# Fixed slots for the lane stages of a convolution, Mamba, attention and experts kernel

## The chip, the cores and the metric

The kernel runs on one core of a Trainium2 chip. The metric is the device time of one execution in microseconds (us). The median of three runs of the kernel before is 5564.33 us (5563.74 to 5565.13).

## The reference

The input x has 4 images of 128 channels and 64x64 pixels, in float32. Two layers follow each other. Cut to what matters:

```python
# layer 0, on the group-normed x, channels last; added to x
xn  = ln(x);  y = xn + fc2(gelu(ln(conv3x3_depthwise(xn))))
u   = ln(y)                                    # 4 chunks of 32 channels, one Mamba each
xin, z = split(u @ in_proj.T);  xin = silu(conv1d(xin))
dt, Bm, Cm = split(xin @ x_proj.T)             # 16 states
delta = softplus(dt @ dt_proj.T + b)
h_t = exp(delta*A) * h_(t-1) + delta*Bm*xin    # along 4096 pixels
m   = (sum_n h*Cm + D*xin) * silu(z) @ out_proj.T + skip*u
x   = x + ln(xn + m) @ proj.T + b
# layer 1, tokens of 128 channels
t = t + attention(ln(t))                       # 4 heads, 4096 x 4096 scores per image
t = t + top2_of_8_experts(ln(t))
```

## The kernel before, in words

An image is cut into NB = 8 blocks of BLK = 512 pixels, so there are 32 blocks. The Mamba scan of one block is 2 halves of 128 partitions (p) with NST = 16 states (n) each. One such (block, p, n) is a unit, and the main loop (lines 1223 to 1270) takes one unit in each turn. A turn is called a slot: 32 slots to a block, 1024 in all. The order in which each engine gets its instructions is the order in which this Python code emits them: `queued` (line 428) ties each instruction to the one before it on its engine.

A slot emits, in this order:

1. `fetched` (732), the DMA of the rows B and C for the unit three slots ahead, on SP; the copy of the last scan's end state, on ACT; `decayed` (742), the exp `da` for the unit two slots ahead, on ACT.
2. One group of attention (line 943): two key tiles of 128 against 1024 queries, that is 4 matmuls `sc` on PE and 2 exps `pT` of 128x1024 on ACT. The matmuls of the probabilities with the values (`weighted`, 960: 8 matmuls `av`) come in the next slot.
3. `scan` (747) on DVE: `h` = rows times `du`, the scan over `h`, and `hc` = rows times `h`. From slot ALONE = 128 (line 1220) on, two neighbours' `hc` are added on POOL, and PE adds the sum into `y`, once in two slots (line 1257).
4. Stages of two lanes, X and Y. All the rest of the work hangs on them. A task is a generator, and each `yield` ends half a stage. `advance(lane, second)` (1137) runs one half: in each slot the second half of X (line 1250, so that of the stage begun in the slot before), the first half of Y, then the `y` matmul, the second half of Y (1263), the `av` matmuls of the group before, and the first half of X (1267). So a lane does one stage per slot, mostly PE in one half and DVE or ACT in the other.

The tasks of Y, for block k, stand in a queue filled ahead (lines 1190 to 1208): `in1` = `inputs(k, p=1)` (3 stages), `y0` = `first_norm(k+2)` (5 stages), `xn` = `conv(k+1)` (13 stages), `in0` = `inputs(k+1, p=0)` (3 stages); at the end of an image also `group_norm` (539). The tasks of X are `closed(k)` (769, 11 stages: output projection, two layer norms, q, k, v of the attention), put in front as soon as block k is scanned (line 1262), and `finished` (1010, called "out", 16 stages: one block of attention output, router, experts), which may begin only in slots 2 to 17 of a block (lines 1148 to 1152). `in1` of block k waits for the scan of block k-1, that is for slot 1 of block k; `in0` of the next block waits for the scan of half p=0, slot 17. `inputs` and `closed` exclude each other by `held` (683, 798). Each lane has one PSUM bank for its matmuls (`work`, 487).

Which task is next is asked in `advance`; apart from the gates above a lane runs as fast as one stage per slot:

```python
if tasks[0][0][0] == "out" and slot < len(units) + 4 and not 2 <= slot % (2 * NST) < NST + 2:
    return False
key, stages, _ = tasks.popleft()
running[lane] = key, stages(lane) if callable(stages) else stages
```

`until` (1165) runs both lanes without slots where an input is needed at once (three slots ahead, line 1227). After slot 1023 the rest of the attention and of the `out` tasks runs alone.

Inside the stages, these names matter: `normalised` (502) is 4 bn_stats and 4 bn_aggr on DVE (`st`, `mv`), then 4 small operations on POOL (`rs`, `shift`), a half without work, and 4 scalings of 128x128 on ACT (`xt`). `inputs` (679) has matmuls in its first stage, then `xin` and `zs` (silu) on ACT with a table load on either side; in its second stage more matmuls, then `bc`, `e`, `ln`, `delta` on ACT, again with two table loads; in its third five operations on POOL (lines 721 to 725, ending in `du`). `conv` does the 9 taps on DVE for images 1 to 3 (line 623), on PE for image 0. In `finished`, `aT` (1025) is multiplied on DVE and used by 4 matmuls with `wp`; the router's top-2 search (1070 to 1078) is 16 small operations on DVE whose result `pr` is transposed on PE; four pairs of experts take a `share` on DVE and a pair of matmuls each (1115 to 1126).

Of the kernel before, what the change touches and what calls it, by code (L numbers as in the profile page):

```python
# [24 lines left out]
NST = 16  # L25
# [11 lines left out]
def conv_mamba_attn_moe_kernel(ctx: ExitStack, tc: tile.TileContext, t: dict):  # L37
    nc = tc.nc
    x, out = t["x"], t["out"]
    B, _, L = x.shape  # L40
    NB = L // BLK
# [61 lines left out]
    with (  # L103
# [20 lines left out]
        for i, (w, bias) in enumerate(((wqn, bqn), (wkn, bkn))):  # L124
            for h in range(NH):
# [9 lines left out]
                k = NH * i + h  # L135
# [10 lines left out]
        norm = bd.tile([1, 2 * NH + 1], F32, name="norm")  # L146
# [317 lines left out]
    def flush():  # L464
        for entry in outgoing:
            entry[0] -= 1
            if entry[0] == 0:
                sync.dma_start(out=entry[1], in_=entry[2])
        outgoing[:] = [entry for entry in outgoing if entry[0]]
# [69 lines left out]
    def group_norm(b):  # L539

        gst = small.tile([P, NB, 6], F32, name="gst", bufs=1)
        ahead = [load_x(x[b], i, "xg") for i in range(2)]
        yield
        yield
        for i in range(0, NB, 2):
            now = ahead
            if i + 2 < NB:
                ahead = [load_x(x[b], i + 2 + u, "xg") for u in range(2)]
            yield
            for u in range(2):  # L550
                vector.bn_stats(out=gst[:, i + u, :], in_=now[u])
            yield
        gmv = small.tile([P, 2], F32, name="gmv", bufs=1)
        vector.bn_aggr(out=gmv, in_=gst)
        ps = work("Y")
        mm(ps[:, 0:1], gmat, gmv[:, 0:1])
        yield
        gm = small.tile([P, 1], F32, name="gm", bufs=2)
        vector.tensor_copy(gm, ps[:, 0:1])
        gd = small.tile([P, 1], F32, name="gd", bufs=1)  # L560
        vector.tensor_sub(gd, gmv[:, 0:1], gm)
        gv = small.tile([P, 1], F32, name="gv", bufs=1)
        vector.scalar_tensor_tensor(gv, gd, gd, gmv[:, 1:2], ALU.mult, ALU.add)
        yield
        ps = work("Y")
        mm(ps[:, 0:1], gmat, gv)
        yield
        gr = small.tile([P, 1], F32, name="gr", bufs=2)
        vector.tensor_scalar_add(gr, ps[:, 0:1], EPS)
        gpsimd.tensor_tensor(gr, gr, mhalf[:, 0:1], ALU.pow)  # L570
        group_of[b] = gm, gr
        yield

    def first_norm(b, i, lane):

        gn = load_x(x[b], i, "gn")
        yield
        gm, gr = group_of[b]
        yield
        yield  # L580
        vector.tensor_scalar(gn, gn, gm, gr, ALU.subtract, ALU.mult)
        yield
        ps = transposed(lane, by_tile(gn))
        yield
        xt = yield from normalised(lane, by_tile(ps))
        ps = transposed(lane, xt).rearrange(IMAGE, w=IMG)
        yield
        y0 = mix.tile([P, ROWS + 2, IMG + 2], F32, name="y0", bufs=4)
        gpsimd.memset(y0[:, :, 0:1], 0.0)
        gpsimd.memset(y0[:, :, IMG + 1 : IMG + 2], 0.0)  # L590
        inner = slice(1, 1 + IMG)
        scalar.activation(y0[:, 1 : 1 + ROWS, inner], ps, AF.Identity, bias=lnb, scale=lnw)
        if i == 0:
            gpsimd.memset(y0[:, 0, inner], 0.0)
        else:
            above = y0_of[b, i - 1]
            scalar.activation(
                above[:, ROWS + 1, inner], ps[:, 0, :], AF.Identity, bias=lnb, scale=lnw
            )
            gpsimd.tensor_copy(y0[:, 0, inner], above[:, ROWS, inner])  # L600
        if i == NB - 1:
            gpsimd.memset(y0[:, ROWS + 1, inner], 0.0)
        y0_of[b, i] = y0
        yield
# [528 lines left out]
    lanes, done, running = {"X": deque(), "Y": deque()}, set(), {}  # L1133

    inside = {"X": False, "Y": False}

    def advance(lane, second):

        if inside[lane] != second:
            return False  # L1140
        while True:
            if lane not in running:

                tasks = lanes[lane] if lanes[lane] or slot < len(units) else lanes["X"]
                if not tasks or not all(k in done for k in tasks[0][2]):
                    return False

                if (
                    tasks[0][0][0] == "out" and slot < len(units) + 4
                    and not 2 <= slot % (2 * NST) < NST + 2  # L1150
                ):
                    return False
                key, stages, _ = tasks.popleft()
                running[lane] = key, stages(lane) if callable(stages) else stages
            key, stages = running[lane]
            try:
                next(stages)
                inside[lane] = not second
                return True
            except StopIteration:  # L1160
                assert not second
                done.add(key)
                del running[lane]

    def until(key):
        while key not in done:
            flush()
            count = len(done)
            moved = [
                advance(*half) for half in (("X", True), ("Y", False), ("Y", True), ("X", False))  # L1170
            ]
            assert any(moved) or len(done) > count, key

    blocks = [(b, i) for b in range(B) for i in range(NB)]

    def before(k, n):

        return [("freed", *blocks[k - n])] if k >= n else []
# [3 lines left out]
    def upper(k):  # L1182
        b, i = blocks[k]
        if i == 0:
            Y.append((("group", b), group_norm(b), []))
        if k != 1:
            Y.append((("y0", b, i), first_norm(b, i, "Y"), before(k, 4)))

    X.append((("y0", *blocks[1]), first_norm(*blocks[1], "X"), [("y0", *blocks[0])]))
    for k in range(-2, len(blocks)):  # L1190
        if 0 <= k:
            b, i = blocks[k]
            Y.append((("in", b, i, 1), inputs(b, i, 1), [("scan", *blocks[k - 1], 1)] if k else []))
        if k + 2 < len(blocks):
            b, i = blocks[k + 2]
            if k + 2 == 0 or i > 0:
                upper(k + 2)
        if 0 <= k + 1 < len(blocks):
            b, i = blocks[k + 1]
            below = [("y0", b, i + 1)] if i < NB - 1 else []  # L1200
            Y.append((("xn", b, i), conv(b, i), before(k + 1, 3) + below))
            Y.append((
                ("in", b, i, 0), inputs(b, i, 0),
                before(k + 1, 2) + ([("scan", *blocks[k], 0)] if k >= 0 else []),
            ))

        if 0 < k + 2 < len(blocks) and blocks[k + 2][1] == 0:
            upper(k + 2)
# [9 lines left out]
    units = [(b, i, p, n) for b, i in blocks for p in range(2) for n in range(NST)]  # L1218

    ALONE = NB // 2 * 2 * NST  # L1220
    rows, decays, old, due = {}, {}, None, deque()
    even, y_of, waiting, slot = None, {}, None, 0
    while slot < len(units) or due or waiting or left or later or lanes["X"] or running:
        flush()

        for ahead in range(slot if slot == 0 else slot + 3, min(slot + 4, len(units))):
            until(("in", *units[ahead][:3]))
            rows[ahead] = fetched(*units[ahead])
# [7 lines left out]
        group = next(groups, None)  # L1236
        if slot < len(units):
# [3 lines left out]
            b, i, p, n = unit  # L1241
# [5 lines left out]
            else:  # L1247
                gpsimd.tensor_add(even, even, hc)
                due.append((slot + 2, unit, even, n == 1))
        advance("X", True)  # L1250
        advance("Y", False)
        while due and due[0][0] <= slot:
            _, unit, term, first = due.popleft()
            b, i, p, n = unit
# [22 lines left out]
    with tc.If(nc.values_load(general[0:1, 0:1]) > 0):  # L1277
# [4 lines left out]
        with tc.For_i(0, B, 1) as b:  # L1282
# [3 lines left out]
                out=t_tok.rearrange("p k c -> p (k c)"),  # L1286
# [97 lines left out]
```

## Time and profile before

| what | value |
|---|---|
| median of the runs | 5564.33 us |
| profiled execution, its own time | 5562.85 us |
| its span, first to last instruction | 5561.1 us |
| busy: PE, DVE, ACT, POOL | 4907.1, 4182.2, 3897.4, 2208.9 us |
| granted TensorE clock, mean | 0.951 |
| slots 0 to 1023 (first to last scan on DVE) | 102.8 to 4969.2 us |
| a block, blocks 8 to 29 | 146.5 to 170.8 us, mean 158.9 us |
| attention groups left after the last slot | 136 of 1024 |

Times are of one profiled execution; "idle before" is the time an engine stood still just before an instruction and the releaser is what it had waited for. Nearly all instructions bear line 445, the helper that records the order, so groups are told apart by the names of their tiles. A slot is found in the trace by its `da` on ACT, its `h` on DVE, and its four `sc` on PE. DVE and ACT may be ahead of PE or behind it in slots.

### The profile page before, as it was taken

How to read it: one execution, taken by the hardware profiler on the slowest of the kernel's cores; microseconds unless marked ns; L12 is line 12 of the kernel's file. 1: busy time of each engine (PE TensorE's matmuls, PEld its weight loads, DVE VectorE, ACT ScalarE, POOL GpSimd, SP SyncE). 2: the span in 40 equal slices, each digit the busy share in tenths (PEclk: the TensorE clock that was granted, in tenths of full speed). 3: DMA queues.
4: the chain of work that ended last, by engine and by line, in shares of the span. 5: the costliest groups of instructions: out<-in, count | busy, mean ns of one | idle time of the engine just before them, and what ended most of it. 6: DMA issues, size and time to landing. Idle time of an engine off the chain costs nothing.

```text
span 5561.1 us, 61179 instructions
## 1 busy us (share of the span) xinstructions
PE 4907.1 (88%) x17866; PEld 2045.2 (37%) x17866; DVE 4182.2 (75%) x6275; ACT 3897.4 (70%) x5989; POOL 2208.9 (40%) x1917
## 2 busy tenths in 40 slices
PE   4667798999899899999999999999899899999997
PEld 2223333333333333333333333333333333344443
DVE  4888778888887888888888888887888788862221
ACT  3455677788777777777877777777777777765553
POOL 2333445445434445444544444444544444421100
PEclk7778899999999999999999999999999999999998
DMA  2456566666665667667765667667765666754542
GB/s 92 169 172 193 185 205 230 215 222 229 228 206 192 228 201 255 216 204 243 249 208 193 209 214 242 219 210 234 249 207 196 207 221 203 249 193 168 168 146 67
DMA packets 451704, 1131.52 MB, mean 203 GB/s; under 512 B 51985, under 2 KB 135330, under 8 KB 451362
## 3 DMA queue, kind: packets, MB, share of 16 engines
q1 hardware_dynamic: 450194, 1126.74, 60.6%
q8 instruction: 144, 2.36, 0.2%
q14 instruction: 198, 1.62, 0.1%
q10 hardware_dynamic: 1168, 0.80, 0.0%
HBM read 967.12 MB, written 143.39 MB: 200 GB/s over the span
## 4 chain that ended last, share of the span: by engine, by line
PE 46%; DVE 18%; ACT 13%; DMA 7%; POOL 7%; issue 7%; SPq 1%; DVEq 0%; ACTq 0%; POOLq 0%
PE av L445 17%; PE sc L445 10%; DVE h L445 9%; PE ps_X L445 8%; PE ps_Y L445 6%; PE y L445 5%; ACT pT L445 4%; ACT xt L445 3%; ACT L445 2%; DMA rows<-bcd 2%; POOL rsY L445 2%; DMA ks<-kd 2%; DVE hc L445 2%; POOL rsX L445 1%; DVE cm L445 1%
## 5 line engine op out<-in xcount | busy, mean ns | idle before, releaser
L445 ACT ACTIVATE pT<-sc 128x1024 f32<-128x1024 f32 x2048 | 1982.2, 1021 | 965.6 <-PE sc L445 963.8
L445 PE MATMUL av<-pT,v 128*64 128x512 f32 x8192 | 2006.7, 611 | 3.7 <-ACT avs L445 3.5
L445 DVE TENSOR_TENSOR_SCAN h<-da,state,h 128x512 f32<-128x512 f32 x896 | 1339.2, 1495 | 106.7 <-ACT da L445 12.5
L445 PE MATMUL sc<-qs,ks 128*128 128x512 f32 x4096 | 1310.8, 440 | 110.9 <-ACT pT L445 55.0
L445 POOL TENSOR_TENSOR hc<-hc 128x512 f32<-128x512 f32 x448 | 641.6, 1434 | 1829.3 <-DVE hc L445 1669.9
L445 PEld LDWEIGHTS sc<-qs,ks 128*128 128x128 f32 x4096 | 716.7, 193 | 795.0 <-ACT pT L445 267.0
L445 PEld LDWEIGHTS av<-pT,v 128*64 128x64 f32 x8192 | 501.6, 137 | 1201.7 <-issue 1121.8
L445 DVE TENSOR_TENSOR h<-rows,du 128x512 f32<-128x512 f32 x1024 | 828.6, 809 | 65.0 <-POOL du L445 29.3
L445 DVE TENSOR_TENSOR hc<-rows,h 128x512 f32<-128x512 f32 x1024 | 807.7, 789 | 79.4 <-DVE h L445 2.3
L445 ACT ACTIVATE da<-delta,amat 128x512 f32<-128x512 f32 x1024 | 749.3, 732 | 15.8 <-DVE h L445 11.7
L445 PE MATMUL y<-hc,ident 128*128 128x512 f32 x1152 | 655.3, 656 | 68.3 <-DVE hc L445 37.7
L445 ACT ACT_TABLE_LOAD x319 | 409.3, 1283 | 18.1 <-PE ps_Y L445 13.0
L445 ACT COPY state<-h 128x1 f32<-128x1 f32 x896 | 175.3, 196 | 178.7 <-DVE h L445 178.3
L445 PEld LDWEIGHTS y<-hc,ident 128*128 128x128 f32 x1152 | 217.2, 206 | 208.9 <-DVE hc L445 74.1
L445 POOL TENSOR_TENSOR avs<-avs,prev 128x512 f32<-128x512 f32 x96 | 145.8, 1518 | 341.8 <-ACT avs L445 258.7
L445 POOL TENSOR_SCALAR rsY<-mvY 128x4 f32<-128x4 f32 x100 | 60.8, 608 | 490.4 <-DVE mvY L445 486.0
L445 DVE TENSOR_TENSOR share<-share,xf 128x1024 f32<-128x1024 f32 x128 | 180.6, 1411 | 92.2 <-DMA share<-sharesX 58.5
L445 PE MATMUL ps_X<-share,w_ew 128*128 128x512 f32 x432 | 215.9, 622 | 24.6 <-DVE share L445 24.5
L445 ACT ACTIVATE xt<-ps_Y,shiftY,rsY 128x128 f32<-128x128 f32 x380 | 143.0, 462 | 124.9 <-POOL shiftY L445 117.4
L445 ACT COPY avs<-av 128x512 f32<-128x512 f32 x160 | 94.1, 588 | 162.4 <-PE av L445 133.8
L445 POOL TENSOR_SCALAR du<-e 128x512 f32<-128x512 f32 x64 | 151.2, 2362 | 140.9 <-ACT e L445 140.8
L445 DVE TENSOR_TENSOR_SCAN h<-da,h 128x512 f32<-128x512 f32 x128 | 182.9, 1429 | 15.4 <-ACT da L445 2.6
(234 smaller groups left out, 4642.2 us busy)
## 6 DMA issues: line engine op xcount, KB each, us to landing
rows<-bcd SPq DMA_DIRECT2D x1024, 512.0 KB
ks<-kd SPq DMA_DIRECT2D x192, 512.0 KB
qs<-qd SPq DMA_DIRECT2D x161, 512.0 KB
share<-sharesX SPq DMA_DIRECT2D x108, 512.0 KB
v<-vd SPq DMA_DIRECT2D x192, 256.0 KB
ks<-kd SPq DMA_DIRECT2D x128, 256.0 KB
avd<-avs SPq DMA_DIRECT2D x96, 256.0 KB
prev<-avd SPq DMA_DIRECT2D x96, 256.0 KB
```

The costliest lines, as they stand in the source:

```text
L445: return lambda *args, **kw: queued(op(*args, **kw))
```

## The change

`phases` gives each task a list of slots, one for each of its stages: stage number j may not begin before slot 32 * period + PHASES[kind][j]. It holds from slot 128 on, does not hold inside `until`, and not for the Y tasks in the last two blocks of an image's eight (where the next image's group norm has its place). A task that is late isn't put back: its stages then follow one per slot until it is on its list again. In the queue of Y, `y0` of block k+2 now stands ahead of `in1` of block k, for the blocks 2 to 7 of an image.

Stage by stage, in slots of a block (before: as the trace shows it for a block inside an image with an `out` task):

| task | before | after |
|---|---|---|
| y0 (5) | 5 to 9 | -3, -2, -1, 0, 1 |
| in1 (3) | 2, 3, 4 | 2, 3, 4 |
| xn (13) | 10 to 22 | 5, 6, 7, 9 to 12, 17 to 22 |
| in0 (3) | 23, 24, 25 | 23, 25, 28 |
| closed (11) | 1, 2, then 3 to 11 | 1, 2, then 4 to 12 |
| out (16) | 12 to 27 | 13, 15 to 18, 20, 21, 22, 24 to 31 |

```diff
+    PHASES = {
+        "y0": (-3, -2, -1, 0, 1),
+        "in1": (2, 3, 4),
+        "xn": (5, 6, 7, 9, 10, 11, 12, 17, 18, 19, 20, 21, 22),
+        "in0": (23, 25, 28),
+        "closed": (1, 2, 4, 5, 6, 7, 8, 9, 10, 11, 12),
+        "out": (13, 15, 16, 17, 18, 20, 21, 22, 24, 25, 26, 27, 28, 29, 30, 31),
+    }
+    rushing = [False]
+
+    def phases(key):
+
+        kind = key[0]
+        if kind == "out":
+            period = slot // (2 * NST)
+        elif kind == "group":
+            return None
+        else:
+            ahead = {"y0": 2, "xn": 1, "in": 1 - key[-1], "closed": -1}[kind]
+            period = NB * key[1] + key[2] - ahead
+            if kind != "closed" and period % NB >= NB - 2:
+                return None
+        kind = f"in{key[-1]}" if kind == "in" else kind
+        return [2 * NST * period + n for n in PHASES[kind]]
...
-                running[lane] = key, stages(lane) if callable(stages) else stages
-            key, stages = running[lane]
+                stages = stages(lane) if callable(stages) else stages
+                running[lane] = key, stages, deque(phases(key) or ())
+            key, stages, times = running[lane]
+            if not second and times:
+                if ALONE <= slot < min(times[0], len(units)) and not rushing[0]:
+                    return False
+                times.popleft()
...
     for k in range(-2, len(blocks)):
+        norm = k + 2 < len(blocks) and (k + 2 == 0 or blocks[k + 2][1] > 0)
+
+        if norm and k > 0 and blocks[k + 2][1] > 1:
+            upper(k + 2)
+            norm = False
         if 0 <= k:
             b, i = blocks[k]
             Y.append((("in", b, i, 1), inputs(b, i, 1), [("scan", *blocks[k - 1], 1)] if k else []))
-        if k + 2 < len(blocks):
-            b, i = blocks[k + 2]
-            if k + 2 == 0 or i > 0:
-                upper(k + 2)
+        if norm:
+            upper(k + 2)
```

`until` sets `rushing[0]` while it runs the lanes.

More of the change, by code (lines that the diff above doesn't have):

```diff
@@ L1168, in until @@
             count = len(done)
+            rushing[0] = True
             moved = [
@@ L1171, in until @@
             ]
+            rushing[0] = False
             assert any(moved) or len(done) > count, key
```

## The prediction

> **What bounds the kernel now.** First the page.
>
> ```profile
> span 5561.1 us, 61179 instructions
> PE 4907.1 (88%) x17866; PEld 2045.2 (37%) x17866; DVE 4182.2 (75%) x6275; ACT 3897.4 (70%) x5989; POOL 2208.9 (40%) x1917
> PEclk7778899999999999999999999999999999999998
> ```
>
> PE is the busiest, with no stage that lacks it. Then the table of windows: blocks 8 to 29, and what comes after the last slot (columns: stretch, length, busy PE, PEld, DVE, ACT, POOL, clock, DMA share, GB/s).
>
> ```profile
> 1173.50:4669.90 3496.40, 3185.29 (x11901) 1328.82 (x11898) 2889.03 (x4233) 2650.09 (x4109) 1577.67 (x1338) 0.97 0.66 219
> 4969.20:5561.00 591.80, 546.27 (x2165) 236.94 (x2164) 145.66 (x401) 308.63 (x381) 47.32 (x68) 0.95 0.40 134
> ```
>
> In these 22 blocks PE is idle for 3496.4 - 3185.3 = 311 us, 14.1 a block. The trace's clock record adds 177 us at half speed there, 161 of them with PE busy, which cost some 80 us (3.7 a block). These 391 us are all that an order of stages can win in the stretch. Who PE waited for there:
>
> ```profile
> PE ps_X L445 <- DVE aT L445: 64.4, 17, 5.6
> PE ps_Y L445 <- ACT xt L445: 40.1, 36, 2.5
> PE sc L445 <- ACT pT L445: 37.5, 74, 2.9
> PE ps_X L445 <- DVE prX L445: 29.8, 17, 2.7
> PE ps_X L445 <- ACT xt L445: 25.6, 38, 5.4
> PE ps_X L445 <- DVE share L445: 24.5, 21, 1.7
> PE sc L445 <- DMA ks<-kd: 24.5, 8, 7.1
> PE y L445 <- POOL hc L445: 20.3, 20, 2.6
> ```
>
> All but the DMA are waits of or behind lane stages. Last, block 19 cut at PE's slots: 2 and 3; 4 to 9; 10 to 13; 14; 28 to 31.
>
> ```profile
> 2919.40:2932.60 13.20, 13.20 (x47) 4.88 (x45) 10.42 (x10) 12.91 (x18) 3.81 (x3) 1.00 0.52 140
> 2932.60:2962.80 30.20, 25.24 (x105) 10.75 (x104) 22.15 (x44) 24.12 (x44) 25.15 (x24) 1.00 0.50 163
> 2962.80:2978.60 15.80, 15.80 (x65) 6.76 (x63) 14.52 (x19) 10.64 (x17) 1.27 (x1) 1.00 0.85 274
> 2978.60:2986.80 8.20, 4.73 (x22) 2.83 (x21) 7.89 (x11) 3.47 (x6) 1.66 (x1) 0.90 0.99 330
> 3055.90:3069.80 13.90, 13.90 (x54) 5.47 (x52) 13.10 (x15) 10.55 (x16) 3.15 (x2) 1.00 0.51 170
> ```
>
> PE is never idle in slots 0 to 3, 10 to 13 and 28 to 31, but loses 5.0 us in 4 to 9 and 3.5 in slot 14, where DVE works for 7.89 of 8.20 us. Slots 28 to 31 hold hardly any lane work. I repeated the cut over 15 blocks (9 to 13, 17 to 21, 25 to 29). Mean PE idle per block: 13.7 us, of it slot 14: 4.1; slot 9: 1.5; slot 20: 1.5; slot 4: 1.1; slot 26: 1.1; slot 5: 0.9; slot 7: 0.7. Half clock: 7.7 us, of it 4.8 in slots 14 and 15, 1.4 in slot 9.
>
> **What the Trainium skill says.** "TensorE: Matmul & The Clock Gate", Part 1: the PE clock is either full or half, and drops after an idle window of about 3.4 us. The trace agrees: the record knows 1.0 and 0.5 only, in stretches of 3.4 us or multiples, and half of that time follows the 4.1 us wait. So such a wait costs about half more than it lasts. "SBUF — State Buffer", on the shared port pair: a DVE operation with two SBUF inputs and a POOL operation shut each other out. The trace agrees in kind: the scan takes 1.28 us alone and 1.50 in the mean, and 2.1 in slots where POOL works. "ScalarE: Activation LUTs", What ACT_TABLE_LOAD costs: about 1283 ns a load. Here 319 loads took 1283 ns in the mean; the change keeps their number. "Perfetto Trace Analysis", Optimization Strategy, advises interleaving regimes with different busiest engines, which is the mechanism in question; no run here shows its size.
>
> **The change part by part.** No instruction is added or removed, so I keep a running lag of DVE and of ACT behind PE, slot by slot, with prices from the groups by shape. Without lanes, a slot costs ACT 0.73 (da) + 2 x 1.02 (pT) + 0.20 = 2.97 us; DVE 2.75 (between 0.68 + 1.28 + 0.69 undisturbed and 0.81 + 1.50 + 0.79 in the mean); PE 3.0, or 3.9 with `y` (quiet slots of the cut). Of a slot with y the 3.9 is sc 1.28, y 0.86, av 1.96. Check on the kernel before, ACT in slots 2 and 3: 2 x 2.97 + 4 loads 5.13 + xin, zs, bc, e, e, ln, delta 4.47 = 15.5 against PE's 6.8 + 6.3. ACT starts at -0.4 and should end at +2.0; the cut shows +2.5, and 1.1 idle on PE. So I let PE stand still for what exceeds a lag of 2.5. DVE is mostly 2 to 5 us ahead.
>
> *Slot 14 (out against the taps).* Before, slots 10 to 14 hold taps, hi/lo, vst and aT together: on DVE 5 x 2.75 + 2.8 + 3.1 + 2.3 + 2.4 + 1.5 = 25.9 against PE's 17 + 3.1 of lanes, so the lead is used up and `wp` waits for `aT`. After, taps are in slots 5 to 10, hi/lo in 11 and 12, and DVE has 13 to 15 with 0.7 of lane work: 9.0 against PE's 10.7. It enters slot 16 about 2.7 ahead, and aT (0.68) is ready before PE asks. Gone: 60 of the 64 us, and the clock behind it, 4.8 half-speed us x 0.5 x 0.9 busy in 20 blocks with `out`, 43 us. Next to wait in this stretch is xt (below).
>
> *Top-2 search.* 16 operations, 2.7 us, between DVE's slot 20 and PE's same slot. The list puts a free slot between (22, 24): PE asks 5 to 6 us later. Gone: 28 of 29.8.
>
> *y0 out of slots 5 to 9.* X's and Y's norms no longer meet in slot 7 (4.1 us on DVE and 6 us on POOL) and slot 8 (3.7 on ACT). Gone in the 18 blocks where Y's lists hold: slot 9's 1.5 plus half of 1.4, 39 us; slot 7's hc wait 0.7, 13 us. Together with the two above: 183 us.
>
> *y0 into slots 29 to 1.* This is paid for. Its load (SP) at 29, one DMA among some six per slot, keeps 1 1/2 slots to `gn`, as before: nothing. gn 0.72 at 30, transposes and norm at 31 (DVE 1.7, POOL 3.1), xt 1.85 at 0, y 1.3 at 1. ACT in slots 0 and 1: 5.9 + 3.2 = 9.1 against PE's 3.0 + 3.9 + 0.65; so ACT enters slot 2 not at -0.4 but at +1.2. Slots 2 and 3: 15.5 against 6.8 + 5.5 (closed's transposes, 0.8, left for slot 4): 4.4, that is 1.9 over the 2.5, against 1.1 measured before. With shiftY late (ACT waited for it 58 times, 2 us each) it is 2.6. I take 2.4, +1.3 a block x 18 = 24. If the lag isn't covered at all: 4.4, +3.3, 59; if slots 28 to 31 give ACT a real lead: 0.
>
> *closed a slot later.* Its first xt falls in slot 6, at ACT's lag 0.9 + 2.77 + 1.85 = 5.5 against PE's 1.28 + 1.96 = 3.2 (no y there): 2.0 to 2.3, against 1.3 in slots 5 and 6 before: +0.7 x 18 = 13. Its POOL chain now queues behind the five `du` operations (8.9 us from about slot 4): it ends at about 13 us after PE's slot 4, when ACT asks at 12.7. Bounds 0 to 40. Slot 12, hi/lo: +0.5, 9 us. Attention after closed(3) and closed(5) of image 0 begins a slot later: one group goes to the tail, +4 less the 3 it leaves, 1 us.
>
> *out, slots 16 to 31.* xt at 18 now follows gelu (17: two loads 2.6 + 0.8): ready at 0.9 + 2.77 + 1.95 = 5.6 against PE's 4.1: +1.5, less 0.4 before, 20 us. Shares in 28 to 31: DVE 4.2 + 4.9 + 5.6 + 6.6 = 21.3, PE 4.7 + 5.6 + 4.7 + 6.3 = 21.3; `du` at slot 28 slows DVE by some 4 us, its lead is 3: +0.3 over slot 26's 1.1, 5 us (bounds -20, +50). du's new place: POOL runs with DVE, ahead of PE, so delta is there 7.3 us later, before ACT's `da` in slot 30 and the rows' products in 32: nothing, 2 us a block if not.
>
> *in0 spread over 23 to 28.* ACT 19.2 against PE 17.4 in three slots instead of 15.5 against 12.7 in two: under the allowance both times: 0.
>
> Clock after the new waits of 2 us and more: 1 us a block, 18. Added in all: 24 + 13 + 9 + 1 + 20 + 5 + 18 = 90. Blocks 4 to 7, 30 and 31 (X's part only, or the convolution on PE): -12. Sum: -183 + 90 - 12 = -105. From the profiled 5562.85 that is 5458, and 5459 from the median, 1.5 us above it. I say 5458. With the bounds, removed 130 to 200 and added 30 to 150: -170 to +20, so the forecast's own range is 5390 to 5500, where added cost is not at its worst throughout.
>
> **The rivals.** *The stalls move* (chance 0.12): PE waits as often, for xt and pT; only aT's clock loss is won. 43 us less some: 5515 to 5552. For it: ACT's load per block is unchanged and 70% busy. Against: slots 28 to 31 were empty, and slot 14's excess was DVE's. *Nothing moves* (0.06): the lists are only lower bounds; if a task comes late each time, or `until` must rush, the order is the old one: 5560. Against: in1 may begin at slot 2 anyway, and in0 ends at 28, before the rush at 29. *Slower by the pile-up around slot 0* (0.13): shares, du, y0 and in1 follow each other from 28 to 6 without a pause. If ACT's 4.4 stands in full, xt's 2.3 follows, two clock stretches (3.4 x 0.5 each) and the DVE-POOL exclusion adds 5: 15 a block against 3.6 before, +11.5, over the 9 or so removed: 18 x 2.7 = +50, 5610. It decides from 9 us of added waits a block; quiet slots 13 to 15 and 26, 27 speak against that, since the engines catch up there. *All absorbed* (0.05): idle falls to 5 us a block, clock loss nearly gone: -220, 5340.
>
> **How the numbers follow.** Forecast 0.64. Faster by over 0.2% (about what a measurement can tell from no change): 0.64 + 0.12 + 0.05 = 0.81; within: 0.06; slower: 0.13. The range leaves out the slower case, part of no change and the far end: 5380 to 5560.
>
> **What would show it.** Right: the aT and prX waits of PE under 10 us each; slots 14 and 15 without half clock; PE idle in blocks 8 to 29 from 311 to some 230 us; new waits for xt (slots 6, 18) and pT (slot 4). DVE busy unchanged within 2%. Wrong: PE waits in slots 28 to 6 above 10 us a block, or POOL chains that release ACT late each block.

## The result

The changed kernel takes 5530.4 us in the median (5525.61 to 5542.84, 4 runs), the one before 5564.03 us (5555.2 to 5565.13, 4 runs). The ratio is 0.9948 (95% interval 0.9931 to 0.9964): 0.5% faster, about 34 us (29 by the ratio), where 105 had been forecast. The page of the profiled execution (5528.97 us):

```profile
span 5527.2 us, 61228 instructions
PE 4899.4 (89%) x17866; PEld 2044.1 (37%) x17866; DVE 4223.7 (76%) x6275; ACT 3906.2 (71%) x5989; POOL 2212.7 (40%) x1917
PEclk7788899999999999999999999999999999999998
```

Blocks 8 to 29 and the time after the last slot, in the table of windows:

```profile
1164.60:4631.50 3466.90, 3180.10 (x11888) 1324.22 (x11886) 2921.81 (x4224) 2658.09 (x4107) 1580.04 (x1337) 0.97 0.66 221
4929.20:5527.20 598.00, 551.51 (x2182) 239.67 (x2178) 149.45 (x406) 309.86 (x382) 47.05 (x68) 0.96 0.40 135
```

The 22 blocks take 3466.9 us instead of 3496.4: 29 us less, which is most of the gain. PE idle fell only from 311 to 287 us, and the half-speed time rose from 177 to 215 us. The rest after the last slot is 6 us longer. Who PE waited for in these blocks:

```profile
PE ps_X L445 <- ACT xt L445: 91.1, 44, 6.8
PE sc L445 <- DMA ks<-kd: 51.8, 11, 6.9
PE ps_X L445 <- ACT prT L445: 42.0, 20, 2.6
PE sc L445 <- ACT pT L445: 30.8, 50, 4.8
PE ps_X L445 <- DVE lo L445: 12.3, 20, 1.4
PE ps_X L445 <- DVE share L445: 8.9, 6, 1.8
PE ps_X L445 <- ACT xf L445: 7.2, 3, 3.3
...
PE ps_Y L445 <- ACT xt L445: 5.9, 7, 1.8
PE ps_X L445 <- DVE aT L445: 4.9, 6, 1.2
...
PE ps_X L445 <- DVE prX L445: 0.7, 1, 0.7
```

Read against the list of before: the waits for aT (64.4), prX (29.8), Y's xt (40.1) and hc (20.3) are gone. In their place stand X's xt (25.6 before), the keys' DMA (24.5 before) and prT (3.9 before). The waits were mostly exchanged. One of the new ones shows on ACT as well, which waits for the end of POOL's part of X's norm (`shiftX`); the first line is of before, the second of after:

```profile
ACT xt L445 <- POOL shiftX L445: 3.0, 4, 1.3
ACT xt L445 <- POOL shiftX L445: 54.7, 43, 4.2
```

Two of the new waits, in block 19. First slot 6, the timeline of POOL (start, duration, operation, idle time before it):

```profile
2911.24 2.76 POOL L445 TENSOR_SCALAR du<-e 128x512 f32<-128x512 f32 x1 [2.84 <-ACT e L445]
2914.09 1.27 POOL L445 TENSOR_TENSOR du<-e,du 128x512 f32<-128x512 f32 x1
2915.43 1.27 POOL L445 TENSOR_TENSOR ln<-ln,du 128x512 f32<-128x512 f32 x1
2916.78 1.34 POOL L445 TENSOR_TENSOR delta<-delta,ln 128x512 f32<-128x512 f32 x1
2918.20 1.60 POOL L445 TENSOR_TENSOR du<-delta,xin 128x512 f32<-128x512 f32 x1
2919.76 1.73 POOL L445 TENSOR_TENSOR hc<-hc 128x512 f32<-128x512 f32 x1
2921.57 1.02 POOL L445 TENSOR_SCALAR rsX<-mvX 128x4 f32<-128x4 f32 x1
2922.68 1.58 POOL L445 TENSOR_TENSOR rsX<-rsX,mhalf 128x4 f32<-128x4 f32 x1
2924.34 0.54 POOL L445 TENSOR_TENSOR shiftX<-mvX,rsX 128x4 f32<-128x4 f32 x1
2924.96 0.55 POOL L445 TENSOR_SCALAR shiftX<-shiftX 128x4 f32<-128x4 f32 x1
```

and what waits for it, on ACT and then on PE:

```profile
2925.54 1.50 ACT L445 ACTIVATE xt<-ps_X,shiftX,rsX 128x128 f32<-128x128 f32 x4 [1.71 <-POOL shiftX L445]
```

```profile
2927.10 1.11 PE L445 MATMUL ps_X<-ident,xt 128*128 128x128 f32 x4 [2.97 <-ACT xt L445]
```

POOL works without a pause from du to shiftX for 14.3 us. Second slot 25, PE and ACT:

```profile
3009.48 1.07 PE L445 MATMUL ps_X<-xin,w_wbc 128*64 128x512 f32 x2 [2.06 <-ACT prT L445]
...
3014.27 1.12 PE L445 MATMUL ps_X<-prT,w_eb 8*128 8x512 f32 x2
```

```profile
3007.05 1.94 ACT L445 ACTIVATE pT<-sc 128x1024 f32<-128x1024 f32 x2 [0.69 <-PE sc L445]
3008.87 0.56 ACT L445 COPY prT<-ps_X 8x512 f32<-8x512 f32 x1
3010.59 0.58 ACT L445 COPY bc<-ps_X 64x512 f32<-64x512 f32 x1 [1.16 <-PE ps_X L445]
```

in0's first matmul of the stage writes X's bank, from which ACT copies prT only after this slot's two exps. The wait is for the bank, not for data, and all of PE stands still for 2.06 us.

The 15 blocks of the prediction, cut into parts; per block, in us: length / PE idle / PE busy at half speed. In a few of the blocks a slot or two have no group of attention, so some borders are estimates and the figures are good to a few tenths.

| slots | before | after |
|---|---|---|
| 0 to 3 | 19.5 / 0.2 / 0.5 | 20.4 / 0.7 / 0.0 |
| 4 to 12 | 42.9 / 5.2 / 1.8 | 43.3 / 5.6 / 3.1 |
| 13 to 22 | 51.1 / 7.0 / 4.1 | 43.2 / 3.3 / 1.9 |
| 23 to 27 | 30.2 / 1.5 / 0.5 | 28.2 / 2.2 / 2.5 |
| 28 to 31 | 14.5 / 0.2 / 0.0 | 20.9 / 0.5 / 0.0 |
| sum | 158.2 / 14.1 / 6.8 | 156.1 / 12.3 / 7.6 |
| last two blocks of an image (14, 15, 22, 23, 30), sum | 162.7 / 14.9 / 9.5 | 163.8 / 16.0 / 12.2 |

Lengths of parts also differ because lane work moved between them; idle and half-speed time can be compared.

### The profile page after: what moved, and what is told of

It is laid out like the page before. It is cut to its first block, busy times and chain, and to the rows that moved or that the text cites. A ratio compares the mean times of both kernels' runs of the same rounds, so it can differ in the third digit from the quotient of the medians.

```text
span 5527.2 us, 61228 instructions
## 1 busy us (share of the span) xinstructions
PE 4899.4 (89%) x17866; PEld 2044.1 (37%) x17866; DVE 4223.7 (76%) x6275; ACT 3906.2 (71%) x5989; POOL 2212.7 (40%) x1917
## 4 chain that ended last, share of the span: by engine, by line
PE 48%; DVE 17%; ACT 10%; POOL 8%; DMA 8%; issue 6%; SPq 1%; DVEq 0%; ACTq 0%; POOLq 0%
PE av L445 18%; PE sc L445 11%; PE ps_X L445 9%; DVE h L445 9%; PE ps_Y L445 6%; PE y L445 5%; DMA rows<-bcd 3%; ACT pT L445 3%; DMA ks<-kd 2%; ACT xt L445 2%; POOL du L445 2%; DVE hc L445 2%; POOL rsX L445 2%; ACT L445 1%; DVE cm L445 1%
## 5 line engine op out<-in xcount | busy, mean ns | idle before, releaser
L445 DVE TENSOR_TENSOR_SCAN h<-da,state,h 128x512 f32<-128x512 f32 x896 | 1289.7, 1439 | 117.7 <-ACT da L445 26.4
L445 POOL TENSOR_TENSOR hc<-hc 128x512 f32<-128x512 f32 x448 | 654.9, 1462 | 1570.2 <-DVE hc L445 1335.2
L445 DVE TENSOR_TENSOR h<-rows,du 128x512 f32<-128x512 f32 x1024 | 852.4, 832 | 152.0 <-ACT state L445 86.5
L445 PE MATMUL ps_X<-ident,xt 128*128 128x128 f32 x368 | 100.4, 334 | 152.4 <-ACT xt L445 140.4
L445 POOL TENSOR_TENSOR rsY<-rsY,mhalf 128x4 f32<-128x4 f32 x100 | 195.0, 1950 | 8.4
```

Source lines behind the costliest of these rows:

```text
L445: return lambda *args, **kw: queued(op(*args, **kw))
```

## The experiments

Times are medians. Ratios are to the kernel before, run on the same chip, with their 95% interval. "From the changed kernel" means against its 5530.4 us; the interval of its ratio, 0.9931 to 0.9964, and that of the run in question say how finely that can be told: a difference under some 13 us (an estimate from both intervals) is not told from none.

**One half of the change alone.** X's lists without Y's:

```diff
-            if kind != "closed" and period % NB >= NB - 2:
+            if kind != "closed":
...
-        if norm and k > 0 and blocks[k + 2][1] > 1:
-            upper(k + 2)
-            norm = False
```

> Lists for closed and out alone; the queue of Y in the old order and without lists. If moving out (and the top-2 search) off the taps is what wins, and y0's new place and in0's spread bring nothing or a loss: 5470 to 5515, with the waits for aT and prX gone, the one for prT absent (in0 is back at slot 24) and the one in slot 6 still there. If y0's move is the winner: 5540 or more.

Measured 5552.68 us, ratio 0.9979 (0.9972 to 0.9986). The number lies in the second forecast, 5540 or more, but its reason, that y0's move is the winner, does not hold: Y's lists alone, below, win no more. The waits for aT and prX fell (17.8 us is left of aT), but slot 6 waits 3.0 us, slot 15 for the taps' result 1.8, and prT 44 us in all: with in0 in slots 23 and 24 its activations leave ACT 3.3 us behind when prT's turn comes. So the wait for prT does not need in0 in slot 25. Y's lists without X's:

```diff
-        if kind == "out":
-            period = slot // (2 * NST)
-        elif kind == "group":
+        if kind in ("out", "group", "closed"):
             return None
...
-            if kind != "closed" and period % NB >= NB - 2:
+            if period % NB >= NB - 2:
```

> Lists and the new order of the queue for Y alone; closed and out run freely as before. Closed's chain is then ahead of du on POOL, out sits at 12 to 27 as before. If the two halves of the change add up, and X's lists alone gave 0.2% of the 0.5%, this gives 0.3%: about 5545 us. If moving the taps ahead is what cures the wait for aT, that wait (69 us) is gone here too and the time is 5490 to 5530; then shares and in0's activations meet again in slots 24 to 27 and the wait for shares is back.

Measured 5556.6 us, ratio 0.9986 (0.9979 to 0.9993). Of aT's wait 42.7 us of 68.7 stay although the taps are out of its way: of DVE's waits before aT, 30.7 us end with the load `inv` (15 of 20 times). So the taps were not the whole cause; X's list, which leaves a slot between loads and use and goes past the taps, does more alone (17.8 us left). In slot 7, from which y0 is gone, PE waits 1.7 us for hc (0.7 before) and in slot 8 1.2 us for X's xt. Of the two forecasts, the first (5545 us, halves that add up) missed by 12 us and the second (5490 to 5530) by more. The halves' 0.21% and 0.14% make 0.35%, which is not told apart from the whole's 0.52% (0.36 to 0.69).

**The wait in slot 6.** The task `closed` goes back by a slot, which puts its norm ahead of du on POOL:

```diff
-        "closed": (1, 2, 4, 5, 6, 7, 8, 9, 10, 11, 12),
+        "closed": (1, 2, 3, 4, 5, 6, 7, 8, 9, 10, 11),
```

> closed's third to eleventh stage go back one slot (1, 2, 3, ... 11); all else as in the changed kernel. Theory A (POOL's queue): the wait for xt in slot 6 comes from the norm's POOL chain standing behind the five du operations of the same slot 4; with closed early the chain stands ahead of them. PE's wait for X's xt falls from 140 us to about 80, ACT's wait for shiftX from 55 us (in blocks 8 to 29) to under 10, and 26 blocks win 2 to 3 us each: 5450 to 5480 us. Theory B (ACT is late in slots 4 to 6 because y0 loads slots 0 and 1): the wait moves to slots 4 and 5 and the time stays within 10 us of 5530.

Measured 5523.51 us, ratio 0.9940 (0.9922 to 0.9958): the time is that of the changed kernel. PE's wait for X's xt fell to 83 us as theory A says, but the time did not follow: PE now waits 1.8 us for hc in slot 7 and 1.0 in slot 8, and slots 4 to 12 take 43.3 us as in the changed kernel. Theory B had the time right, but not the place: only 0.6 us moved to slot 5. Next, du a slot later instead:

```diff
-        "in1": (2, 3, 4),
+        "in1": (2, 3, 5),
```

> Only the third stage of in1, the five POOL operations that end in du, goes from slot 4 to slot 5; closed stays late. Theory A: the norm's POOL chain is now ahead of du, so the wait for xt in slot 6 falls from 3.2 us to under 1 and its half clock goes: 5450 to 5480 us, like the run with closed early. Theory B: no change, 5520 to 5540.

Measured 5536.36 us, ratio 0.9962 (0.9948 to 0.9975). Slot 6's wait fell from 3.2 to 1.5 us and its clock mostly recovered, yet slots 9, 11 and 12 wait 1.4, 0.6 and 1.1 us instead of 0.4, 0.1 and 0.4: DVE enters slot 9 1.8 us behind PE, not 0.8 ahead, and a tap takes 1.09 us there in the mean instead of 0.99. Both theories failed as put, A in the time and B in the wait: the order on POOL makes the wait in slot 6, but is not alone in setting the length of the stretch. Is it DVE, then?

```diff
-            else:
+            elif k < 2:
                 vector.scalar_tensor_tensor(hr, y0, w, hr, ALU.mult, ALU.add)
```

> The changed kernel with taps 3 to 9 of the convolution left out for images 1 to 3 (7 operations of 0.9 us on DVE per block, 24 blocks); all else in its place. Theory C: in slots 4 to 12 DVE is what ends last (47 us of DVE time for PE's 43), so every wait of PE that is taken away there comes back as another one; without the taps the stretch falls from 43.3 to about 39 us a block and the whole by 80 to 130 us: 5400 to 5450. Rival D: the stretch is set by the ACT and POOL chain of the norm (xt, shiftX), and DVE has room: less than 1.5 us a block, 5495 or more.

Measured 5486.64 us, ratio 0.9862 (0.9842 to 0.9882): 122 us less DVE work gives 44 us, and slots 4 to 12 still take 42.4 us, with slot 6's 3.2 us untouched. Theory C is wrong alone. Rival D's bound of 1.5 us a block holds for these slots (0.9 us), its 5495 us does not; the rest of the gain lies elsewhere (slots 13 to 22 take 42.4 us instead of 43.2). Both edits together, du in slot 5 and the taps left out:

> du in slot 5 instead of 4, and taps 3 to 9 of images 1 to 3 left out. Apart these gave +6 and -44 us against the changed kernel. Theory G (two limits side by side in slots 4 to 12, the POOL chain at slot 6 and DVE's taps behind it, each covering the other): together they give clearly more than the sum, 5420 to 5460. If the two only add up: 5485 to 5500.

Measured 5439.43 us, ratio 0.9780 (0.9758 to 0.9802): 91 us from the changed kernel, where +6 and -44 make 38. Slots 4 to 12 take 39.8 us. Two limits stand side by side there, du in front of the norm on POOL and the taps on DVE, and either one hides what taking away the other would bring. POOL's work bears on both, on the first by its queue and on the second if it slows DVE. So it is made shorter:

```diff
-        lost = du
-        gpsimd.tensor_scalar(lost, e, 1.0, -1.0, ALU.add, ALU.add)
-        gpsimd.tensor_sub(lost, e, lost)
-        gpsimd.tensor_add(ln, ln, lost)
```

> The changed kernel without the first three of the five POOL operations of each third stage of inputs (a correction to the logarithm in delta, 5.6 of 8.9 us, so delta is a little less exact); nothing moves. Theory A2 (POOL's du ahead of the norm's chain sets slot 6, and its sharing with DVE sets slots 9 to 12): slot 6's wait falls from 3.2 us to about 1, its half clock goes, slots 9 and 12 ease: -3 us in 26 blocks, 5440 to 5470. Theory D2 (ACT alone is late after in1): slot 6 keeps its wait, 5520 or more.

Measured 5436.17 us, ratio 0.9771 (0.9753 to 0.9789): -94 us, more than forecast. Slot 6's wait fell from 3.2 to 1.5 us, and slots 4 to 12 take about 2.3 us less. The waits in slots 9 and 12, which theory A2 expected to ease, did not (0.5 and 0.4 us). The same edit on the kernel before:

> The kernel before, without the same three POOL operations of inputs as in the short-du run (delta a little less exact). In the changed kernel that gave 94 us. If the new order's own conflict (the norm's chain behind du) is what they price, the old order wins much less, only du's sharing with DVE in slots 10 to 13 and 4 to 6: 20 to 45 us, 5520 to 5545. If POOL's load is simply dear anywhere: 80 us or more here too, below 5485.

Measured 5443.98 us, ratio 0.9790 (0.9773 to 0.9806): -117 us. So POOL's chain is dear in either order, and its price is not the new order's own. Blocks 8 to 29 of both short-du runs, first on the changed kernel, then on the one before (same columns as above):

```profile
1135.70:4549.00 3413.30, 3156.39 (x11888) 1313.69 (x11886) 2848.37 (x4223) 2655.01 (x4106) 1310.82 (x1205) 0.98 0.67 224
1141.90:4552.10 3410.20, 3161.89 (x11905) 1323.65 (x11906) 2881.79 (x4233) 2651.63 (x4109) 1341.40 (x1205) 0.98 0.66 224
```

The shorter chain wins 54 us there in the new order and 86 in the old (some 30 more of each come before block 8). The 29 us that the lists had won in these blocks are then gone: 3413 against 3410 us (one profiled execution each). The waits of the second run in blocks 8 to 29:

```profile
PE ps_X L445 <- DVE aT L445: 64.8, 17, 5.6
PE sc L445 <- ACT pT L445: 37.1, 73, 2.9
PE ps_X L445 <- DVE prX L445: 29.8, 17, 2.7
PE sc L445 <- DMA ks<-kd: 27.3, 10, 6.9
PE ps_X L445 <- ACT xt L445: 24.6, 36, 5.4
PE ps_Y L445 <- ACT xt L445: 18.1, 30, 1.8
```

aT and prX stand as before; Y's xt fell from 40.1 to 18.1 us, and hc (20.3) is gone. These are the two waits that the prediction had put down to the norms of X and Y meeting in slots 7 and 8. With y0 still in its old place hc goes and Y's xt is more than halved when du is shorter.

**The wait in slot 25.** in0's second stage a slot earlier:

```diff
-        "in0": (23, 25, 28),
+        "in0": (23, 24, 28),
```

> Only the second stage of in0 goes from slot 25 to slot 24. Theory A (X's PSUM bank): in slot 25 its first matmul writes the bank that the experts' prT is still to be copied out of by ACT in that same slot, and PE waits; in slot 24 the bank is free. PE's wait for prT falls from 43 us to under 5, slot 25 loses 1.8 us of idle time and 2.3 us of half clock in 22 blocks: about -60, 5470 us. Rival: ACT's load of 15.5 us in slots 23 and 24 against PE's 12.7 brings a wait for pT that takes most of it back: 5510 to 5530.

Measured 5541.8 us, ratio 0.9965 (0.9953 to 0.9977). The bank is free, and PE waits for prT all the same (44.6 us): ACT enters slot 25 3.3 us behind. What waits is now prT's own matmul, all 22 times; in the changed kernel it was in0's matmul in 15 of 22. Neither forecast held in its number; the rival was right that ACT's burst takes the gain back. Next, prT moved ahead and in0 behind it:

```diff
-        "in0": (23, 25, 28),
+        "in0": (23, 26, 28),
-        "out": (13, 15, 16, 17, 18, 20, 21, 22, 24, 25, 26, 27, 28, 29, 30, 31),
+        "out": (13, 15, 16, 17, 18, 20, 21, 22, 23, 24, 26, 27, 28, 29, 30, 31),
```

> in0's second stage goes to slot 26, and the out stages that end in ACT copies (prT, res) go to 23 and 24 with their copies in slots 24 and 25, so that prT, res and in0's activations no longer meet in one slot or one PSUM bank. Theory E: the 2.0 us wait and 2.3 us of half clock in slot 25 are the price of that meeting, 3 us in some 20 blocks: 5465 to 5485, PE's wait for prT under 10 us. Rival: the wait turns into one for pT or res after the burst, as it did with in0 at 24: 5520 or more.

Measured 5517.35 us, ratio 0.9909 (0.9885 to 0.9934). prT's wait is gone, but slots 27 and 28 wait 1.3 us for pT after the burst: near the rival. Next, in0 right before the experts' shares:

```diff
-        "in0": (23, 25, 28),
+        "in0": (24, 27, 28),
```

> in0's first stage goes to 24 and its second to 27; out stays. Theory H: in0's second stage is 5.8 us of ACT in one slot, which cost nothing before because PE had the experts' shares (5.6 us slots) beside and behind it; in the changed kernel it stands in slot 25, ahead of slots with almost no PE lane work. At 27 it lies ahead of the shares again, and clear of prT and res. The 2.0 us and the half clock of slot 25 go and no wait for pT takes their place: -3 us in 20 blocks, 5460 to 5485. Rival: delta comes late, since du starts after slot 27's activations, and ACT's da in slot 30 waits for POOL: 5520 to 5550.

Measured 5497.05 us, ratio 0.9885 (0.9866 to 0.9903): -33 us, where theory H had 45 to 70. Its waits in blocks 8 to 29:

```profile
PE ps_X L445 <- ACT xt L445: 96.3, 47, 7.3
PE sc L445 <- DMA ks<-kd: 56.5, 13, 6.4
PE sc L445 <- ACT pT L445: 31.9, 49, 4.8
...
PE ps_X L445 <- ACT prT L445: 11.3, 8, 2.4
```

prT fell from 42.0 to 11.3 and pT did not rise (30.8, now 31.9): behind the burst PE has shares to do. Slots 23 to 27 went from 28.2 to 25.1 us, with idle 2.2 to 0.5. The rival, late delta, did not show: ACT's da waits for POOL in none of these blocks.

**The keys.** The loads of `out` go behind the stores of `closed`:

```diff
-        "out": (13, 15, 16, 17, 18, 20, 21, 22, 24, 25, 26, 27, 28, 29, 30, 31),
+        "out": (15, 16, 17, 18, 19, 20, 21, 22, 24, 25, 26, 27, 28, 29, 30, 31),
```

> out begins at 15 instead of 13 and goes on with 16, 17, 18, 19, 20 (from 20 on as in the changed kernel). Theory F: PE's waits for keys in slot 15 or 16 (85 us in all) come from out's three loads in slot 13 standing ahead of the keys behind closed's stores of slots 11 to 13; the loads now follow the keys. Keys' wait from 85 to 40 to 60 us, xt in slot 19 no longer behind gelu (1.0 us a block): 5480 to 5510. Rival: the loads only collide with the next keys or rows: 5525 to 5540.

Measured 5515.69 us, ratio 0.9908 (0.9888 to 0.9928). The keys' wait fell from 85 to 66 us and xt behind gelu is gone; aT waits 1.0 us in slot 17 for loads that now come late. In slot 16, where the keys' wait of blocks 8 to 29 falls, it is halved (47.5 to 23.7 us, with 9.2 new in slot 18), so the loads ahead of the keys are about half of its cause. The time lies between the forecasts, and 15 us are at the edge of what can be told.

**Together.** First two moves, in0 at 24, 27, 28 and out from 15 on:

> As the run with three moves, but closed as in the changed kernel (1, 2, 4 to 12). The two single moves gave 33 and 15 us: 5475 to 5490 if they add.

Measured 5484.29 us, ratio 0.9858 (0.9841 to 0.9874): 46 us, about the sum of 33 and 15. Then closed a further slot later as well, so that its norm comes to POOL when du is nearly through:

```diff
-        "in0": (23, 25, 28),
-        "closed": (1, 2, 4, 5, 6, 7, 8, 9, 10, 11, 12),
-        "out": (13, 15, 16, 17, 18, 20, 21, 22, 24, 25, 26, 27, 28, 29, 30, 31),
+        "in0": (24, 27, 28),
+        "closed": (1, 2, 5, 6, 7, 8, 9, 10, 11, 12, 13),
+        "out": (15, 16, 17, 18, 19, 20, 21, 22, 24, 25, 26, 27, 28, 29, 30, 31),
```

> Nothing left out: in0 at 24, 27, 28; out from 15 on (15 to 22, 24 to 31); closed from its third stage a slot later still (1, 2, 5 to 13), so that its norm reaches POOL when du is done, with out's loads behind its stores. If the three causes (du ahead of the norm, in0's activations in an empty slot, keys behind out's loads) are apart and each move cures its own: 33 + 15 + some 40 us from the changed kernel, 5435 to 5465. If du's sharing with DVE rules the stretch in whatever order: 5470 to 5500.

Measured 5414.64 us (5410.54 to 5416.63), ratio 0.9733 (0.9717 to 0.9750): 147 us faster than the kernel before and 116 faster than the changed one, with the whole computation in place. Its blocks 8 to 29, and their first waits:

```profile
1148.00:4515.00 3367.00, 3139.48 (x11890) 1313.24 (x11888) 2943.63 (x4224) 2653.48 (x4106) 1592.22 (x1337) 0.98 0.67 227
```

```profile
PE ps_X L445 <- ACT xt L445: 55.3, 36, 5.7
PE sc L445 <- ACT pT L445: 36.3, 48, 3.3
PE sc L445 <- DMA ks<-kd: 30.7, 13, 7.0
PE ps_X L445 <- DVE aT L445: 21.9, 14, 3.3
```

PE idle is 227.5 us instead of 286.8, half-speed time 130 instead of 215. closed's one slot is worth 70 us here, part of it in the last two blocks of the images (164.4 to 160.4 us a block). Slot 7 still waits 2.0 us for xt, so how much of the 70 us is the order on POOL and how much the easier stretch of DVE stays open.

## Why the prediction was wrong

The direction was right and the size was three times too large. 5530 us lies inside the outer range, 5380 to 5560, but not in the forecast's own, 5390 to 5500. It lies in that of a rival: "the stalls move", 5515 to 5552, which had been given a chance of 0.12. The steps that failed are two in the main: the 52 us for taking y0 out of slots 5 to 9, where the stretch kept its length, and the zero for in0 in slot 25, which cost some 33 us. By the prediction's own steps:

- *Slot 14* and *top-2 search*: right in their numbers. aT went from 64.4 to 4.9 us (60 had been said to go), prX from 29.8 to 0.7, half speed in slots 13 to 22 from 4.1 to 1.9 us a block. The reason given for aT was only in part right: with the taps moved and out left free, 42.7 of 68.7 us of its wait stay. "Next to wait" was not xt alone but the keys, 24.5 to 51.8 us. About half of that comes from out's loads ahead of them in the DMA queue; that PE's stop for aT had covered it before is likely, but no run shows it.
- *y0 out of slots 5 to 9*, 52 us: the step that failed in its reason. With what was added for closed and hi/lo, slots 4 to 12 were to be 1.7 us a block shorter; they stayed (42.9 and 43.3 us; idle 5.2 and 5.6). The named waits went and others came. Two things hold this stretch: du's chain on POOL, 8.9 us from slot 4 on, and DVE's taps, which POOL's work slows. The old order with a shorter chain loses the wait for hc, and more than half of Y's for xt, with y0 in place (the short-du run on the kernel before); the new order without y0 there has hc again in slot 7 (Y's lists alone). So the waits were handed on, not removed. How much of POOL's part is its queue and how much its slowing of DVE stays open.
- *y0 into slots 29 to 1*, 24 us: over-priced. ACT enters slot 4 3.1 us late instead of 2.5, but PE idles 1.1 us there as before; some 0.5 us a block appears in slots 0 to 3.
- *closed a slot later*, 13 us with 40 as its bound: the local wait was mis-sized. Slots 5 and 6 idle 3.6 us instead of 1.3. The working compared the end of POOL's chain, 13 us after PE's slot 4, with ACT's request at 12.7 and let it go; in block 19 it was 13.9 us and ACT had asked 1.7 us before, with xt's own 1.5 us still to come before PE could go on. But this wait is not what the time lost: closed put back alone moved it to slots 7 and 8 and won 7 us, no more than can be told from none.
- *in0 spread over 23 to 28*, 0: a term put at nothing. Moving in0 alone, to 24, 27 and 28, won 33 us, the most of any single move made on the changed kernel. The running lag allows ACT 2.5 us, but only the exps have that allowance. A lane stage has none: PE asks for it 1.3 to 3.2 us after the slot begins, and ACT gets to it some 3 us after. Slot 25 has 1.8 us idle and 2.3 us at half clock (0.3 and 0.2 before). The working of the lag never asked which X stage shared the slot and the bank.
- *Clock after the new waits*, 1 us a block: too small. Slots 5 to 7 and slot 25 together run 5.9 us a block at half speed instead of 0.9, which costs some 2.5 us (an estimate: half of the difference, with PE busy all the time).
- *Last two blocks of an image*: the aT and prX gains were counted for them. There Y runs free, in0 has its activations in slots 18 and 19, and X's list now puts xt and xf into these same slots: in blocks 14 and 22 PE waits 3.3 us for xf in slot 19 and runs 5.1 us in the mean at half speed. These blocks became 1.1 us longer, where some 5 had been counted as won (the gains of X's lists less their costs). No run moves this meeting alone.
- *out, slots 16 to 31*: right. PE's wait for xt in slot 18 came, somewhat smaller than put down (18.6 us in all; 1.5 us in 18 blocks would be 27), and slots 28 to 31 idle 0.5 us a block.

What would have shown it was half right: aT, prX, the clock of slots 14 and 15 (0.6 us at half speed, 4.8 before) and DVE's busy time (+1%) came as said; PE idle of 230 us did not (287). And one of the two signs of being wrong came: POOL chains that release ACT late, 54.7 us for shiftX in blocks 8 to 29, where it had been 3.0.

## What to carry to other kernels

A wait that a profile names is the last in its stretch, not the only one: ask of each what is late next, and count a stage's move on every queue it uses, here on POOL's too. When taking away one wait does nothing, take away two: du's move on POOL and DVE's taps together gave 91 us, where alone the second gave 44 and the first nothing. And the right list can be worth more than its forecast: with three stages moved, the same idea gave 147 us. Work that loads one engine in a burst belongs where the others have work of their own behind it, and nothing that is needed at once should stand behind it on that engine.

## What the runs showed of the hardware

In the clock records of the kernel before, the changed one and the one with three moves, every stretch begins on one grid with steps of 3.41 us (within 9 ns). A wait of about 2 us was enough for half clock, if it fell whole into one step. In 13 of the 15 blocks of the changed kernel PE idles 2.06 to 2.34 us in slot 25. In ten of them the wait lies within one step, and the next step runs at half speed; in the other three a border cuts it, into parts of at most 1.64 us, and no half step follows. Slot 25 of blocks 12 and 19 has the same wait of 2.06 us:

```profile
1906.03:1917.67 11.64, 9.58 (x32) 3.71 (x29) 6.20 (x6) 8.03 (x12) 5.49 (x5) 0.85 0.47 121
3006.25:3016.23 9.98, 7.92 (x31) 3.21 (x29) 6.02 (x7) 7.57 (x12) 5.09 (x4) 1.00 0.34 106
```

The first, at a mean clock of 0.85, takes 1.66 us longer. So the same wait costs 2.06 us or about 3.7, by where it falls. Over blocks 8 to 29 of the changed kernel, of the full-speed steps in which PE idled 1.9 us or more in all, 40 of 42 were followed by a half-speed step; of those with less than 1.3 us, 1 of 873; between, 11 of 37. The prediction took an idle window of about 3.4 us for the drop; here idle time of 1.9 us within such a step was nearly always enough.

DVE's operations take longer where POOL works: a tap takes 0.86 us in the mean of the 15 blocks before, 0.99 in the changed kernel, where the taps lie beside du, and 0.90 there with the shorter du. In blocks 8 to 29 of the changed kernel it takes 0.74 us where no POOL operation runs beside it and 1.04 where one does.
